# A four-layer graph network on one core: the order of the first statistics, and the last four batches' attention by another division of engines

## The chip, the cores and the metric

The kernel runs on one core of a Trainium2 chip. A core has five engines that run side by side, each with its own queue in program order: TensorE (PE in the profile, with its weight loads as PEld), VectorE (DVE), ScalarE (ACT), GpSimd (POOL) and SyncE (SP), which here only issues DMA transfers. The metric is the device time of one execution in microseconds, the median of several runs. Before the change it is 1679.53 us (3 runs, 1678.21 to 1679.84).

## The reference

There are 32 batches of 512 nodes with 128 features each (`x`), and one sparse symmetric 512x512 matrix `adj`. Four layers follow each other, each of the form `x = x + layer(...)`:

```python
# layer 0: graph convolution, out of h = relu(layernorm(x))
A_hat = adj + eye(n)
d = sum(A_hat, -1) ** -0.5
out = einsum('nm,bmc->bnc', d[:, None] * A_hat * d[None, :], h) @ W.T + b

# layer 1: gated recurrence, 5 steps from h = relu(layernorm(x)); both matrices are adj
m_in = m_out = einsum('nm,bmd->bnd', adj, h)
av = concatenate([m_in, m_out], -1)
u3 = h @ u3_w.T + u3_b
z = sigmoid(av @ w3_w.T + w3_b + u3)
r = sigmoid(av @ w4_w.T + w4_b + u3)
hv = tanh(av @ w5_w.T + w5_b + (r * h @ u5_w.T + u5_b))
h = (1 - z) * h + z * hv

# layers 2 and 3: attention over the edges, from relu(layernorm(x))
h = einsum('bnf,fo->bno', relu_ln_x, W)
e = leaky_relu((h @ a_src)[:, :, None] + (h @ a_dst)[:, None, :], 0.2)
alpha = softmax(where(edge, e, -inf), -1)
out = einsum('bij,bjo->bio', alpha, h)        # layer 2 ends in elu(out)
```

As both halves of `av` are the same, the kernel uses the sum of the two halves of `w3_w`, `w4_w` and `w5_w`.

## The kernel before

The kernel records its operations, each with an engine, an estimated cost, a due time and the values it reads and writes. A small list scheduler then runs the records through a model with those costs, deals out buffers, and emits the instructions of each engine in the order that comes out. The costs and due times are therefore part of the program: changing them changes the order on all engines, not only near the change.

```python
DELAY = {"PE": 0.25, "ACT": 0.2, "DVE": 0.15, "POOL": 0.15, "SP": 2.4, "AQ": 2.4}
...
}, 172, 0.1)                     # how urgent an operation with a long tail becomes
MM, MM1, TURN = 0.86, 0.235, 0.117
V, A = 0.61, 0.62
```

At the start, `adj` is turned, its degrees are summed, `anT` (the normalised matrix of layer 0) is made, and then the factors of `adj` that the recurrent layer's product uses. That product takes two batches at once and seven instead of eight block products; its factors are sums and differences of `adj`'s quarters.

```python
for c in range(C):               # C = 4 chunks of 128 rows
    op("PE", C * TURN, -800, turn_adj, r=[adj_sb[c], ident], w=[p])
    op("ACT", A, -800, ... nc.scalar.copy(adjT.t[:, :, c * P:(c + 1) * P], p.t) ...)
    op("DVE", V, -800, ... nc.vector.reduce_sum(deg.t[:, c:c + 1], adj_sb.t[:, c, :]) ...)
op("DVE", 0.1, -799, ... add 1 to deg)
op("POOL", 1.0, -1000, ... dinv = deg ** -0.5)
op("PE", C * TURN, -798, turn_dinv, r=[dinv, ident], w=[drow])

def scale_rows():                # one operation: four rows, then four diagonals
    for m in range(C):
        nc.vector.scalar_tensor_tensor(anT.t[:, m, :], adjT.t[:, m, :], dinv.t[:, m:m + 1], flat(drow.t), ...)
    for m in range(C):
        nc.vector.scalar_tensor_tensor(block(anT.t, m), ident.t, dinv2.t[:, m:m + 1], block(anT.t, m), ...)
op("DVE", 4 * 0.7 + 4 * 0.25, -797, scale_rows, ..., w=[anT])

half_adj = fixed([P, 7, 2, 2 * P], "half_adj", 7)
# factors 0, 3, 5: copies of quarters; 2, 1, 4, 6: differences; all on DVE, due -795
...
ws = ...                         # w4, w3, w5: halves added on DVE, then w3 - w4; PE turns the sums
```

Layer norm and the first layer:

```python
def norm_stats(b, due):          # bn_stats x4, bn_aggr x4, +eps on DVE; power -0.5 on POOL
def norm_relu(b, y, due):
    mv, rstd = norm_stats(b, due)
    op("DVE", ... off = -mean * rstd)
    for c in range(C):
        op("ACT", 0.32, due, ... nc.scalar.activation(chunk(y, c), xb.t[:, c, :], AF.Relu,
                                                      bias=off..., scale=rstd...))

def gcn(b, due):                 # called with due = 5 b - 10 or so
    norm_relu(b, y, due)
    op("DVE", V, due + 1, ... x += b0)
    m = product(y, anT, due + 1) # four 128x512 matmuls and a copy by ACT
    op("PE", C * MM1, due + 2, out_mm, ...)
    op("DVE", V, due + 2, ... x += result)
```

Attention, for the last four batches (`near`), which turn their tile on PE where the other batches go through DRAM:

```python
norm_relu(b, y, due)
if near:
    pT = to_features(y, due + 1, gT)                         # PE turns y
    op("DVE", V, due + 1, ... nc.vector.tensor_copy(gT, pT))
else:
    shuttle(y, ...)
for a in range(2):
    op("PE", 2 * MM1, due + 1.5, heads, ...)                 # h and its scores
    op("ACT", 0.1, due + 1, ... exp of the scores)
    op("DVE", 0.335, due + 1.5, ... nc.vector.tensor_mul(h, q, exp))
if near:
    op("PE", C * TURN, due + 2, spread, ...)                 # scores of all nodes on every partition
    op("ACT", A, due + 2, ... copy to row)
for j in range(C):
    op("DVE", 0.68, due + 3, ... e[j] = max(row, score j) * mask)
for a, p in enumerate(ps):
    for c in range(2):
        def mix(...):                                        # one receiving chunk, all four senders j
            for j in range(C):
                nc.tensor.matmul(..., e.t[:, j, i * P:(i + 1) * P], h.t[:, j, :D + 1], start=(j == 0), stop=(j == C - 1))
        op("PE", C * MM1, due + 4, mix, r=[e, h], w=[p])
    op("DVE", ... reciprocal of the sums)
    # layer 2: v = p * rden on DVE, then exp on ACT and two DVE operations for elu
    # layer 3: x = p * rden + x on DVE, then the write to DRAM
```

Of the kernel before, what the change touches and what calls it, by code (L numbers as in the profile page):

```python
# [12 lines left out]
ALU = mybir.AluOpType  # L13
# [29 lines left out]
class Plan:  # L43
# [3 lines left out]
    DELAY = {"PE": 0.25, "ACT": 0.2, "DVE": 0.15, "POOL": 0.15, "SP": 2.4, "AQ": 2.4}  # L47
# [104 lines left out]
def gnn_stack(ctx: ExitStack, tc: tile.TileContext, a: dict, out: bass.AP):  # L152
# [47 lines left out]
    }, 172, 0.1)  # L200
    op = plan.op
    MM, MM1, TURN = 0.86, 0.235, 0.117
    V, A = 0.61, 0.62
# [27 lines left out]
    for c in range(C):  # L231
        e, q = (("SP", nc.sync), ("ACT", nc.scalar))[c % 2]
        op(e, 0.9, -1001, lambda c=c, q=q: q.dma_start(adj_sb.t[:, c, :], adj[c * P:(c + 1) * P, :]),
           w=[adj_sb[c]], delay=2.6 + c)
# [10 lines left out]
    op("DVE", 0.25, -800, lambda: nc.vector.tensor_scalar_add(b0.t, b0.t, -1.0), w=[b0])  # L245
# [15 lines left out]
    adjT = Val("e", C)  # L261
    deg, dinv = fixed(SMALL, "deg", C), fixed(SMALL, "dinv")
    for c in range(C):
# [7 lines left out]
        op("DVE", V, -800, lambda c=c: nc.vector.reduce_sum(deg.t[:, c:c + 1], adj_sb.t[:, c, :], axis=mybir.AxisListType.X),  # L271
# [5 lines left out]
    anT = fixed([P, C, N], "anT")  # L277
# [12 lines left out]
    def scale_rows():  # L290
        for m in range(C):
            nc.vector.scalar_tensor_tensor(anT.t[:, m, :], adjT.t[:, m, :], dinv.t[:, m:m + 1], flat(drow.t),
                                           op0=ALU.mult, op1=ALU.mult)
        for m in range(C):
            nc.vector.scalar_tensor_tensor(block(anT.t, m), ident.t, dinv2.t[:, m:m + 1], block(anT.t, m),
                                           op0=ALU.mult, op1=ALU.add)
    op("DVE", 4 * 0.7 + 4 * 0.25, -797, scale_rows, r=[adjT, dinv, drow, ident, dinv2], w=[anT])


    half_adj = fixed([P, 7, 2, 2 * P], "half_adj", 7)  # L300
# [4 lines left out]
    def factor(k, out_of, *also):  # L305
        op("DVE", 0.62, -795, lambda: out_of(half_adj.t[:, k]), r=[adjT, *[half_adj[i] for i in also]], w=[half_adj[k]])
    for k, u, n in ((0, 0, 0), (3, 1, 0), (5, 1, 1)):
        factor(k, lambda o, u=u, n=n: nc.vector.tensor_copy(o, quarter(u, n)))
    factor(2, lambda o: nc.vector.tensor_sub(o, quarter(0, 1), quarter(0, 0)))
    factor(1, lambda o: nc.vector.tensor_sub(o, quarter(1, 1), half_adj.t[:, 2]), 2)  # L310
    factor(4, lambda o: nc.vector.tensor_sub(o, quarter(1, 1), quarter(0, 1)))
    factor(6, lambda o: nc.vector.tensor_sub(o, quarter(1, 0), half_adj.t[:, 1]), 1)
# [24 lines left out]
    ws = {k: fixed([P, D], k + "s") for k in ("w4", "w3", "w5")}  # L337
    for k in ("w4", "w3", "w5"):
        op("DVE", 0.25, -700, lambda k=k: nc.vector.tensor_add(ws[k].t, raw[k].t[:, :D], raw[k].t[:, D:]),
           r=[raw[k]], w=[ws[k]])  # L340
    op("DVE", 0.25, -699, lambda: nc.vector.tensor_sub(ws["w3"].t, ws["w3"].t, ws["w4"].t), r=[ws["w4"]], w=[ws["w3"]])

    def transposed(due, *group):

        p = Val("bank")
        t = fixed([P, len(group), P], "wT")

        def turns():
            for i, (v, _) in enumerate(group):
                nc.tensor.transpose(p.t[:, i, :], v.t[:, :D], ident.t)  # L350
        op("PE", len(group) * TURN, due, turns, r=[ident] + [v[0] for v, _ in group], w=[p])
# [7 lines left out]
    w0T = transposed(-750, (w0, 1))  # L359
    gates = transposed(-700, (ws["w4"], 1), (raw["u3"], 1), (ws["w3"], 1), (ws["w5"], 1))  # L360
    u5T = transposed(-690, (raw["u5"], 0.5))
    gats = transposed(-10, (w_aug[2], 1), (w_aug[3], 1))
    gate_b = {}
    for k, u, half in (("w4", "u3", True), ("w3", "u3", True), ("w5", "u5", False)):
        gate_b[k] = fixed([P, 1], "gate_b" + k)
        op("DVE", 0.1, -695, lambda k=k, u=u: nc.vector.tensor_add(gate_b[k].t, raw["b" + k].t, raw["b" + u].t),
           r=[raw["b" + k], raw["b" + u]], w=[gate_b[k]])
        if half:
            op("DVE", 0.1, -695, lambda k=k: nc.vector.tensor_scalar_mul(gate_b[k].t, gate_b[k].t, 0.5), w=[gate_b[k]])
# [26 lines left out]
    def norm_relu(b, y, due):  # L396
# [5 lines left out]
        for c in range(C):  # L402
            op("ACT", 0.32, due, lambda c=c: nc.scalar.activation(  # L403
                chunk(y, c), xb.t[:, c, :], AF.Relu, bias=off.t[:, c:c + 1], scale=rstd.t[:, c:c + 1]),
               r=[xb[c], off, rstd], w=[y[c * len(y.writers) // C]])

# [41 lines left out]
    def product(h, mT, due):  # L448

        p, m = Val("bank"), Val("m")  # L450
        for c in range(C):
            op("PE", MM, due, lambda c=c: nc.tensor.matmul(flat(p.t), chunk(h, c), mT.t[:, c, :], start=(c == 0), stop=(c == C - 1)),  # L452
               r=[h[c] if len(h.writers) > 1 else h, mT], w=[p, m])
# [4 lines left out]
    def gcn(b, due):  # L458
        xb, y = xs[b], Val("y", C)
        norm_relu(b, y, due)  # L460
# [30 lines left out]
    def products(h1, h2, due):  # L491
# [20 lines left out]
        def times(r, item, k, fresh, *also):  # L512
            def two():
                u = part(item).rearrange("p (f l) -> p l f", l=2)
                for l in range(2):
                    nc.tensor.matmul(flat(r.t)[:, :2 * P], u[:, l, :], half_adj.t[:, k, l, :], start=fresh and l == 0, stop=l == 1,  # L516
                                     skip_group_check=not fresh)
            op("PE", HM, due, two, r=[item, half_adj], w=[r, *also])
# [78 lines left out]
    def gat(b, l, due):  # L597
        xb, y, gT, h = xs[b], Val("y", C), Val("gT"), Val("h_gat", 4)
        norm_relu(b, y, due)
# [3 lines left out]
        if near:  # L603
            pT = to_features(y, due + 1, gT)
            op("DVE", V, due + 1, lambda: nc.vector.tensor_copy(
                gT.t.rearrange("p q (c i) -> p q c i", c=C), pT.t.rearrange("p c (q i) -> p q c i", q=Q)), r=[pT], w=[gT])
        else:
# [114 lines left out]
```

## Time and profile before

| | us |
|---|---|
| time, median of 3 | 1679.53 |
| span of the profiled execution | 1677.5 |
| busy PE, DVE, ACT, POOL | 1647.4, 1373.7, 675.1, 142.9 |
| first matmul of the first product of layer 0 | 21.29 |
| first matmul of the recurrent product | 37.49 |
| last addition of a recurrent result into x ends | 1619.1 |
| VectorE's last instruction ends | 1674.1 |

The profile's page gives the busy time of each engine over the whole span; its stages give the same for a stretch of time. The timeline lists instructions in order of time. A line L516 is line 516 of the kernel before; the important ones are L268 (turning adj), L283 (turning dinv), L292 and L295 (anT), L308 to L312 (the factors), L339 and L341 (weight sums), L386, L390 and L393 (statistics of the layer norm), L403 (its activation), L452 (product with anT), L516 (recurrent product), L575 (last addition of the recurrence for the last pair), L605 (copy of the turned tile), L618 (heads), L622 (scaling of h), L632 and L634 (row of scores), L647 (e) and L658 (mix). An fp32 matmul has two records on PE, a turn has one. The busy time of a stage has to be read beside the engine that feeds it: an engine that is full in one stage and half idle in another has different meaning in each.

### The profile page before, as it was taken

The page shows a single profiled execution, that of the slowest core. Times are in us where ns is not written, and L with a number is a line of the kernel's source. Part 1 is how long each engine was busy: PE and PEld are TensorE (multiplying, and loading weights), DVE is VectorE, ACT ScalarE, POOL GpSimd, SP SyncE. Part 2 cuts the span into 40 slices and gives each one's busy share as a digit, 9 for nine tenths or more (in the row PEclk, how much of TensorE's full clock was granted, in tenths as well). Part 3 has the DMA queues.
Part 4 walks back from the last instruction along what each step waited for, and adds up shares of the span by engine and source line. Part 5 has one row for each costly group of instructions (what it writes and reads, how often), then busy time and mean ns, then how long its engine had stood idle before and what let it go on. Part 6 is the DMA issues. An engine that isn't in the chain of part 4 may idle for free.

```text
span 1677.5 us, 23419 instructions
## 1 busy us (share of the span) xinstructions
PE 1647.4 (98%) x7224; PEld 1140.3 (68%) x7224; DVE 1373.7 (82%) x3894; ACT 675.1 (40%) x1458; POOL 142.9 (9%) x136
## 2 busy tenths in 40 slices
PE   6999999999999999999999999999999999999997
PEld 4656667576676676767676676776767767676786
DVE  7867688688887897969988688896978879887887
ACT  4434343525444344342543434344343434334332
POOL 2200001001010010100101010010100001000000
PEclk9999999999999999999999999999999999999999
DMA  5213333242433334243433333424233432424101
GB/s 160 52 40 76 76 88 76 69 130 73 114 88 85 103 97 101 59 105 101 125 83 83 94 94 80 112 75 120 73 95 98 110 83 79 113 76 108 45 14 32
DMA packets 311422, 146.15 MB, mean 87 GB/s; under 512 B 150400, under 2 KB 292864, under 8 KB 311296
## 3 DMA queue, kind: packets, MB, share of 16 engines
q1 hardware_dynamic: 311008, 144.12, 33.9%
q8 instruction: 57, 0.93, 0.2%
q14 instruction: 69, 0.57, 0.1%
q10 hardware_dynamic: 288, 0.52, 0.1%
HBM read 80.48 MB, written 64.08 MB: 86 GB/s over the span
## 4 chain that ended last, share of the span: by engine, by line
PE 95%; DVE 3%; ACT 1%; issue 0%; DMA 0%; POOL 0%; DVEq 0%
PE bank L516 29%; PE bank L658 13%; PE bank L545 8%; PE bank L546 8%; PE bank L552 8%; PE bank L559 8%; PE bank L560 8%; PE bank L452 7%; PE bank L618 3%; PE bank L468 2%; PE bank L419 1%; DVE e L647 1%; PE bank L639 0%; DVE st L386 0%; ACT y L403 0%
## 5 line engine op out<-in xcount | busy, mean ns | idle before, releaser
L516 PE MATMUL bank<-half_adj,S 128*128 128x256 f32 x1280 | 311.1, 380 | 1.3 <-DVE S L503 1.3
L516 PEld LDWEIGHTS bank<-half_adj,S 128*128 128x128 f32 x1280 | 245.3, 196 | 53.3 <-issue 21.1
L393 POOL TENSOR_TENSOR rstd<-ve,mhalf 128x4 f32<-128x4 f32 x128 | 140.4, 1099 | 1497.5 <-DVE ve L391 1186.3
L658 PEld LDWEIGHTS bank<-h_gat,e 128*128 128x128 f32 x2048 | 237.8, 191 | 16.0 <-issue 9.1
L516 PE MATMUL bank<-half_adj,h 128*128 128x256 f32 x960 | 243.6, 380 | 0.9 <-ACT h L579 0.5
L658 PE MATMUL bank<-h_gat,e 128*128 128x129 f32 x2048 | 240.9, 275 | 1.0 <-DVE e L647 0.9
L548 ACT ACTIVATE r<-bank,gate_bw 128x512 f32<-128x512 f32 x160 | 109.7, 685 | 288.8 <-PE bank L546 257.8
L516 PEld LDWEIGHTS bank<-half_adj,h 128*128 128x128 f32 x960 | 183.0, 196 | 39.6 <-issue 18.4
L647 DVE SCALAR_TENSOR_TENSOR e<-row,h_gat,maskT 128x512 f32<-128x512 f32 x256 | 181.0, 742 | 0.1
L403 ACT ACTIVATE y<-x,off,rstd 128x128 f32<-128x128 f32 x384 | 160.3, 484 | 50.8 <-DVE off L400 29.2
L550 DVE SCALAR_TENSOR_TENSOR rh<-r,hT 128x512 f32<-128x512 f32 x160 | 109.8, 687 | 85.6 <-ACT r L548 84.7
L564 DVE TENSOR_TENSOR hv<-hv,hT 128x512 f32<-128x512 f32 x160 | 109.1, 682 | 80.8 <-ACT hv L562 80.3
L545 PE MATMUL bank<-m,wT 128*128 128x512 f32 x320 | 163.7, 593 | 0.3 <-DVE m L536 0.3
L552 PE MATMUL bank<-m,wT 128*128 128x512 f32 x320 | 163.6, 593 | 0.0
L559 PE MATMUL bank<-m,wT 128*128 128x512 f32 x320 | 163.4, 592 | 0.0
L546 PE MATMUL bank<-hT,wT 128*128 128x512 f32 x320 | 163.4, 592 | 0.0
L560 PE MATMUL bank<-rh,wT 128*128 128x512 f32 x320 | 163.4, 592 | 0.0
L562 ACT ACTIVATE hv<-bank,gate_bw 128x512 f32<-128x512 f32 x160 | 109.5, 684 | 133.1 <-PE bank L560 131.0
L554 ACT ACTIVATE z<-bank,gate_bw 128x512 f32<-128x512 f32 x160 | 109.4, 684 | 102.9 <-PE bank L552 96.6
L452 PE MATMUL bank<-anT,y 128*128 128x512 f32 x256 | 125.2, 605 | 3.9 <-ACT y L403 3.9
L386 DVE BATCH_NORM_STATS2 st<-x 128x6 f32<-128x128 f32 x512 | 121.6, 279 | 3.0 <-DMA x<-in_x_dram 2.3
L560 PEld LDWEIGHTS bank<-rh,wT 128*128 128x128 f32 x320 | 60.8, 190 | 76.5 <-issue 68.6
(109 smaller groups left out, 1845.7 us busy)
## 6 DMA issues: line engine op xcount, KB each, us to landing
far<-sq SPq DMA_DIRECT2D x832, 64.0 KB
h<-far SPq DMA_DIRECT2D x248, 128.0 KB
gT<-far SPq DMA_DIRECT2D x56, 256.0 KB
row<-line SPq DMA_DIRECT2D x56, 256.0 KB
x<-in_x_dram SPq DMA_DIRECT2D x32, 256.0 KB
out_dram<-x SPq DMA_DIRECT2D x32, 256.0 KB
h<-far SPq DMA_DIRECT2D x28, 256.0 KB
far_mask<-mask SPq DMA_DIRECT2D x8, 128.0 KB
```

Of the source, the lines that this page charges most:

```text
L386: op("DVE", 0.21, due, lambda c=c: nc.vector.bn_stats(st.t[:, c, :], xb.t[:, c, :]), r=[xb[c]], w=[st[c]])
L393: op("POOL", 1.0, due, lambda: nc.gpsimd.tensor_tensor(rstd.t, ve.t, mhalf.t, ALU.pow), r=[ve, mhalf], w=[rstd])
L403: op("ACT", 0.32, due, lambda c=c: nc.scalar.activation(chunk(y, c), xb.t[:, c, :], AF.Relu, bias=off.t[:, c:c + 1], scale=rstd.t[:, c:c + ...
L452: op("PE", MM, due, lambda c=c: nc.tensor.matmul(flat(p.t), chunk(h, c), mT.t[:, c, :], start=(c == 0), stop=(c == C - 1)), r=[h[c] if len ...
L516: nc.tensor.matmul(flat(r.t)[:, :2 * P], u[:, l, :], half_adj.t[:, k, l, :], start=fresh and l == 0, stop=l == 1, skip_group_check=not fresh)
L545: nc.tensor.matmul(flat(gate.t), gates.t[:, 0, :], flat(m.t), start=True, stop=False)
L546: nc.tensor.matmul(flat(gate.t), gates.t[:, 1, :], flat(hT.t), start=False, stop=True)
L552: op("PE", MM, due + 0.3, lambda: nc.tensor.matmul(flat(gate.t), gates.t[:, 2, :], flat(m.t), start=False, stop=True, skip_group_check=Tru ...
L559: nc.tensor.matmul(flat(cand.t), gates.t[:, 3, :], flat(m.t), start=True, stop=False)
L560: nc.tensor.matmul(flat(cand.t), u5T.t[:, 0, :], flat(rh.t), start=False, stop=True)
L647: op("DVE", 0.68, due + 3, lambda j=j: nc.vector.scalar_tensor_tensor(e.t[:, j, :], row.t, h.t[:, j, D + 1:D + 2], maskT[l].t[:, j, :], op ...
L658: nc.tensor.matmul(pt()[:, c, :D + 1], e.t[:, j, i * P:(i + 1) * P], h.t[:, j, :D + 1], start=(j == 0), stop=(j == C - 1))
```

## The change

What it does:

- The statistics and the activation of the first two batches are due ahead of the factors of adj; the factors come later on VectorE.
- anT is made chunk by chunk, row and diagonal together, and a product's matmul waits for its chunk alone.
- The three factors that were copies of quarters are read from the turned adj in place.
- The sums of the weights' halves are no longer added on VectorE: PE accumulates the halves, turned by a product with the identity (or with minus the identity for w3 - w4).
- The last four batches: the layer norm's scaling goes to VectorE without the relu, the relu goes into the copy of the turned tile, which moves to ScalarE, and so does the scaling of h.
- Their mix runs sender by sender, so that it can begin with the first quarter of e and has little left after the last.
- The scheduler's costs, delays and two constants of urgency are set anew.

The purpose is to begin the first products earlier, to take work off VectorE at both ends, and to shorten what stands behind the last e. The diff, cut to its core:

```diff
-    DELAY = {"PE": 0.25, "ACT": 0.2, "DVE": 0.15, "POOL": 0.15, "SP": 2.4, "AQ": 2.4}
+    DELAY = {"PE": 0.24, "ACT": 0.15, "DVE": 0.12, "POOL": 0.1, "SP": 2.4, "AQ": 2.4}
-    }, 172, 0.1)
+    }, 174, 0.08)
-    MM, MM1, TURN = 0.86, 0.235, 0.117
-    V, A = 0.61, 0.62
+    MM, MM1, TURN = 0.858, 0.224, 0.111
+    V, A = 0.61, 0.585
...
-    adjT = Val("e", C)
+    adjT = fixed([P, C, N], "adjT", C)
-        op("DVE", V, -800, ... reduce_sum
+        op("DVE", 0.66, -801, ... reduce_sum
...
-    anT = fixed([P, C, N], "anT")
+    anT = fixed([P, C, N], "anT", C)
-    op("DVE", 4 * 0.7 + 4 * 0.25, -797, scale_rows, r=[adjT, dinv, drow, ident, dinv2], w=[anT])
+    for m in range(C):
+        op("DVE", 0.7, -797, ... row m, r=[adjT, dinv, drow], w=[anT[m]])
+        op("DVE", 0.26, -797, ... diagonal m, r=[ident, dinv2], w=[anT[m]])
...
-    half_adj = fixed([P, 7, 2, 2 * P], "half_adj", 7)
+    half_adj = fixed([P, 4, 2, 2 * P], "half_adj", 4)
+    PLAIN = {0: (0, 0), 3: (1, 0), 5: (1, 1)}
+    def right(k):
+        return quarter(*PLAIN[k]) if k in PLAIN else half_adj.t[:, FACTOR[k]]
-    factor(...)                  # three copies, four differences, due -795
+    for k, u, v in ((2, (0, 1), 0), (1, (1, 1), 2), (4, (1, 1), None), (6, (1, 0), 1)):
+        op("DVE", 0.62, -6, ... tensor_sub
...
-    op("DVE", 0.25, -700, ... ws[k] = raw[k][:, :D] + raw[k][:, D:]     # three, and one difference
+    minus = fixed([P, P], "minus")
+    op("ACT", 0.25, -900, lambda: nc.scalar.mul(minus.t, ident.t, -1.0), r=[ident], w=[minus])
-                nc.tensor.transpose(p.t[:, i, :], v.t[:, :D], ident.t)
+                for k, (v, at, sign) in enumerate(parts):
+                    nc.tensor.matmul(p.t[:, i, :], v.t[:, at:at + D], sign.t, start=k == 0, stop=k == len(parts) - 1)
...
+    def norm(b, y, due):
+        mv, rstd = norm_stats(b, due)
+        for c in range(C):
+            op("DVE", 0.16, due, ... nc.vector.tensor_scalar(y.t[:, c, :], xb.t[:, c, :], mv.t[:, c, 0:1], rstd.t[:, c:c + 1],
+                                                             op0=ALU.subtract, op1=ALU.mult))
...
-               r=[h[c] if len(h.writers) > 1 else h, mT], w=[p, m])
+               r=[h[c] if len(h.writers) > 1 else h, mT[c]], w=[p, m])
-        norm_relu(b, y, due)
+        norm_relu(b, y, due if b > 1 else 2 * b - 798)
...
         if near:
+            norm(b, y, due)
-            op("DVE", V, due + 1, ... tensor_copy(gT, pT))
+            op("ACT", A, due + 1, ... activation(gT, pT, AF.Relu))
...
+            if near:             # scaling of h
+                op("ACT", 2 * 0.385, due + 1.5, ... two nc.scalar.mul)
+            else:
                 op("DVE", 0.335, due + 1.5, ... tensor_mul)
...
+        if near:
+            for j in range(C):
+                def mix_from(j=j):
+                    for c in range(C):
+                        nc.tensor.matmul(... chunk c of bank c // 2 ..., e.t[:, j, c * P:(c + 1) * P], h.t[:, j, :D + 1],
+                                         start=j == 0 and c % 2 == 0, stop=j == C - 1, skip_group_check=True)
+                op("PE", C * MM1, due + 4, mix_from, r=[e[j], h[j // 2], h[2 + j // 2]], w=[*ps])
```

## The prediction

> **What bounds the kernel now.** I read the page's busy times first, then the same by stages, then PE's waits, then the timeline of the two ends.
>
> ```profile
> PE 1647.4 (98%) x7224; PEld 1140.3 (68%) x7224; DVE 1373.7 (82%) x3894; ACT 675.1 (40%) x1458; POOL 142.9 (9%) x136
> ```
>
> PE is idle for only 1677.5 - 1647.4 = 30.1 us. The stages say where (per stage: length, then busy us and instructions of PE, PEld, DVE, ACT, POOL, then PE's clock, DMA share, GB/s):
>
> ```profile
> 0.00:20.00 20.00, 8.01 (x32) 6.34 (x32) 13.12 (x49) 5.23 (x10) 2.91 (x9) 1.00 0.77 218
> 20.00:40.00 20.00, 18.71 (x61) 10.47 (x62) 17.05 (x90) 11.27 (x28) 7.59 (x8) 1.00 0.40 117
> 40.00:60.00 20.00, 20.00 (x78) 13.07 (x77) 19.36 (x86) 15.16 (x35) 7.25 (x7) 1.00 0.12 34
> ...
> 300.00:500.00 200.00, 200.00 (x890) 139.24 (x890) 166.66 (x465) 82.50 (x182) 15.87 (x15) 1.00 0.39 99
> ...
> 1619.10:1647.40 28.30, 20.60 (x171) 19.17 (x169) 27.74 (x105) 9.55 (x23) 4.88 (x5) 0.96 0.04 11
> 1647.40:1655.20 7.80, 7.52 (x44) 6.92 (x44) 4.49 (x13) 6.10 (x20) 1.60 (x2) 0.70 0.00 0
> 1655.20:1674.20 19.00, 17.11 (x144) 16.34 (x144) 16.73 (x42) 2.01 (x5) 0.00 (x0) 1.00 0.15 43
> ```
>
> From 21.3 to 1516 us PE never stops, so nothing done there can pay except less PE work, and the change does not reduce PE work. What can be had lies in the first 21 us and in the last 58. From 1619.1, where the last recurrent step adds into x, VectorE is nearly full (27.74 of 28.3) and PE is not: the end is VectorE's. PE's longest waits agree:
>
> ```profile
> PE bank L618 <- DVE gT L605: 7.2, 2, 6.7
> PE bank L268 <- DMA e<-in_adj_dram: 4.7, 1, 4.7
> PE bank L452 <- ACT y L403: 3.9, 1, 3.9
> PE bank L350 <- DMA a_pair<-in_L_gnn_a_dst_dram: 2.8, 1, 2.8
> ```
>
> The start in the timeline (start, us from first start to last end, engine, line, operation). L274 is dinv, L283 its turn, L292 anT's rows, L390 the aggregation of batch 0's statistics, L393 its power, L452 the first product:
>
> ```profile
> 9.42 1.66 POOL L274 TENSOR_TENSOR dinv<-deg,mhalf 128x4 f32<-128x4 f32 x1 [8.06 <-DVE deg L273]
> 11.32 1.06 PE L283 MATMUL bank<-ident,dinv 128*128 128x128 f32 x4
> 12.41 2.72 DVE L292 SCALAR_TENSOR_TENSOR anT<-e,dinv,bank 128x512 f32<-128x512 f32 x4 [0.47 <-PE bank L283]
> 18.84 0.37 DVE L390 BATCH_NORM_AGGREGATE mv<-st 128x2 f32<-128x6 f32 x4
> 19.50 1.01 POOL L393 TENSOR_TENSOR rstd<-ve,mhalf 128x4 f32<-128x4 f32 x1 [8.43 <-DVE ve L391]
> 21.29 8.41 PE L452 MATMUL bank<-anT,y 128*128 128x512 f32 x12 [3.93 <-ACT y L403]
> ```
>
> anT is done at 16.2, but batch 0's statistics stand in VectorE's queue behind the factors of adj, so the product waits until 21.29.
>
> **What the skill says.** "TensorE: Matmul & The Clock Gate", part 1, "The HAM clock gate": PE runs at half rate until about 3.4 us of sustained work, and falls back after an idle window. The trace agrees: weight loads of the first product come 0.855 us apart until 27.4 us and 0.43 after it; after the hole before 1647.49 eight 131-wide matmuls take 2.12 us, later eight take 1.06. So each hole costs twice. "VectorE: DVE Perf Modes", "Mode 2x_2P": single-source fp32 operations inside SBUF run at twice the rate, those on PSUM do not. Agrees: the 128x512 copy in SBUF took 421 ns, from PSUM 686. "ScalarE: Activation LUTs", "What ACT_TABLE_LOAD costs": 186 ns + 0.83 ns a column, 93 more per pointer operand; for 128 columns and two pointers 479, and the trace has 484. "PSUM", "The four PSUM rules": the first matmul of a group clears the accumulate bits of its whole bank. That is why the mix by sender starts only the first group of each bank; no run here shows it and no time hangs on it.
>
> **The start, step by step.** Back-to-back distances from the timeline: turn 0.217 cold and 0.11 warm; fp32 matmul two records, so 128 wide 0.43 cold and 0.22 warm, 512 wide 1.71 and 0.857; VectorE 128x512 with two tensors 0.6 to 0.68, bn_stats 0.2, aggregation of four 0.3. In the changed order the four degree sums stand together: 4.61 + 4 x 0.61 = 7.1. With 1.66 for the power dinv is there at 9.1 instead of 11.1. But PE's order is 16 turns of adj (4.72 to 8.2; each in a bank of its own, so the two waits of 0.7 for ScalarE go), then w0 and the sums of w4, w3 and w5, nine matmuls, and only then dinv's turns. Cold that is 3.9 + 0.9, until 13.0; if the clock opens at about 10, until 11.6. I take 12.1: drow is hardly earlier than now (12.4). The weight sums take back what the earlier dinv gave; they are 13 matmuls for 8 turns, 18 records more, 2 to 4 us of PE, at a time when PE would mostly wait.
>
> Then anT 0, off, anT 1, two diagonals: 0.68 + 0.1 + 0.68 + 0.5, so chunks 0 and 1 are there at 14.05, chunks 2 and 3 at 15.9. Batch 0's power runs right after dinv's (9.1 to 10.1), ScalarE has copied the weights by 13.2, and y's first chunk is there at 13.6. First product 14.05 to 17.6, warm if the unbroken work from 4.72 opened the clock. That is 7.2 us earlier in its start. The gain is not kept whole: VectorE, dense from here on, now has the statistics of batch 1, gate sums and factors to do, and PE is fed in pieces. Following the two orders: batch 1's product 19.2 to 23.1, its output matmuls 23.8 to 24.7, the first recurrent product 25.7 (now 37.49), and by 39.5 PE has done 21.7 us of full-speed work since its first product. Now it has done 3.05 by 27.4 and as much as 21.7 at 46.0. Gain 6.5. A check by VectorE: it is idle 10.5 us of the first 60; the change takes 4 weight sums (1.0) and 3 copies (1.2 to 1.6) off it, and about 7 us of idle time stay (the load, the wait for drow). So at most 6. I take **-5**.
>
> **The last four batches.** Per such attention layer VectorE loses the copy from PSUM (0.6), two scalings (0.66) and off (0.1) and gains four normalisations of 128 columns (about 0.14 each: the one 128x128 tensor_scalar kept the next waiting 0.13). So -0.8. ScalarE loses four activations (1.65) and gains one PSUM copy (0.6) and four scalings (some 0.4 each): +0.5, and it is idle there. Mix by sender: after the last e only 4 matmuls remain (0.9) where 13 of 16 did (2.9).
>
> VectorE's work behind the last add into x, from the changed order: 27 e x 0.665 = 18.0; 16 last additions x 0.26 = 4.2; 20 bn_stats 3.9; 20 normalisations 2.8; 6 half products x 0.33 = 2.0; 6 of elu x 0.6 = 3.6; 14 reciprocals 1.1; aggregations and eps 2.3. Sum 37.9; the same sum for now gives 47.9 against 48.96 measured, so 38.7. For waits I find 1.2 (row of the second last layer-2 batch: ScalarE's scalings stand ahead of the row copy), 0.7 and 1.7 (rows of layer 3, the same cause), in all 3.6. So 42.3 us from the last add to VectorE's end, now 55.1: -12.8. Against it: PE has 359 records (40.2 us) behind that add now and 316 (35.4) then. The 4.8 us stand ahead of it, where PE is idle 3.6 us between 1500 and 1619; I let the add come 3.5 later for this. That leaves -9; with a wait or two that I did not see, **-8**. The last write, 3.3 us, stays.
>
> **The middle.** The whole order is dealt anew because costs, delays and the urgency constants changed. Work per batch is the same (the products read adj's quarters in place, 256 columns in a run as in the copies). PE can only lose: **+1**.
>
> Sum: 1679.5 - 5 - 8 + 1 = 1667.5.
>
> **The rivals.** (1) The weight sums keep drow back: clock cold, w5 late, drow at 13, product cold (6.9 us for the first batch). For it: PE stayed cold until 21 now, though with holes. Then the start gains 2, total 1670.5. (2) ScalarE becomes the bound at the end: its queue is in order, and exp, scalings, gT and rows of three batches share it; each scaling ahead of a row delays four e's. For it: at the end some 12 us of its work stand before the last row. Against it: 17.7 busy of 55 now. Then the end gains 4, total 1671.5. (3) The new order opens holes in the middle: VectorE is busy 83% there, and a buffer handed out in another order can stall PE; 0.5% more would be +8 and eat most of it. Against it: PE had none over 1480 us. (4) Both ends come out whole: -6.5 and -12, 1661.
>
> **Range and chances.** Two ends with 2 to 4 us of doubt each and the middle with 2 to 5 on the bad side: 1660 to 1675. PE's busy time sets a floor near 1640, so 2% (1645.9) is out of reach; 2% slower would need a new stall of 45 us. 0.01, 0.98, 0.01.
>
> **What will show it.** First product of batch 0 before 15 us and its clock; dinv's turns after the weight sums, at 11.5 to 13; first recurrent product at 25 to 28. From the last add to VectorE's end 42 to 46 us, no hole of 6.7 us in PE before the last layer's heads, clock there warm. PE idle under 1 us in all between 60 and 1500. The prediction is wrong if the middle shows PE waits of several us, or if drow comes after 14.

## The result, and the profile after

| | before | after |
|---|---|---|
| time, median of 6 runs each, taken in turns on one chip | 1679.68 us | 1668.3 us |
| span of the profiled execution | 1677.5 | 1667.2 |
| first matmul of the first product | 21.29 | 13.57 |
| first matmul of the recurrent product | 37.49 | 25.20 |
| PE idle up to 60 us | 13.28 | 7.37 |
| PE idle from 60 to 1500 us | 0 | 0 |
| PE idle from 1500 us to the end of the span | 16.8 | 14.4 |
| last addition of a recurrent result into x ends | 1619.2 | 1618.58 |
| VectorE's last instruction ends | 1674.1 | 1663.85 |

The ratio after to before is 0.9935, with a 95% interval of 0.9922 to 0.9948. The prediction of 1667.5 us is 0.8 us off. That is not yet a proof of its reasons: it is a sum of three terms, and two wrong terms can cancel.

The stages of the profile after, in the columns used before the change:

```profile
0.00:20.00 20.00, 13.70 (x65) 10.49 (x66) 12.96 (x48) 9.04 (x20) 3.79 (x10) 1.00 0.76 217
20.00:40.00 20.00, 18.94 (x78) 12.45 (x77) 19.47 (x96) 10.90 (x27) 6.20 (x6) 1.00 0.41 119
...
60.00:1500.00 1440.00, 1440.00 (x6173) 989.93 (x6172) 1182.45 (x3255) 585.67 (x1235) 111.68 (x100) 1.00 0.36 90
```

and the last part of it, cut at the last addition into x and at VectorE's last instruction:

```profile
1500.00:1618.58 118.58, 114.78 (x564) 82.19 (x563) 95.80 (x268) 44.73 (x106) 8.83 (x8) 0.99 0.22 58
1618.58:1663.85 45.27, 38.02 (x303) 34.94 (x302) 40.77 (x134) 16.70 (x50) 5.57 (x5) 0.96 0.07 20
```

The middle is as full as it was: PE is busy for all of its 1440 us. Over the span PE's idle time falls from 30.1 to 21.8 us (1667.2 - 1645.4), and its busy time by 2.0, of which the lines below show a part to be cold matmuls that are now warm. Of the 8.3 us of idle time 5.9 lie in the first 60 us and 2.4 behind 1500.

The start, PE and the power of dinv in the timeline after (L347 turns weights, L283 dinv, L464 is the first product, L528 the recurrent one; in brackets the idle time ahead and what ended it):

```profile
7.61 1.02 POOL L274 TENSOR_TENSOR dinv<-deg,mhalf 128x4 f32<-128x4 f32 x1 [6.25 <-DVE deg L273]
8.04 2.20 PE L347 MATMUL bank<-ident,w 128*128 128x128 f32 x10
10.07 0.61 PE L347 MATMUL bank<-minus,w 128*128 128x128 f32 x4
...
10.97 0.60 PE L283 MATMUL bank<-ident,dinv 128*128 128x128 f32 x4
13.57 3.80 PE L464 MATMUL bank<-anT,y 128*128 128x512 f32 x8 [1.55 <-DVE anT L294]
25.20 1.48 PE L528 MATMUL bank<-adjT,h 128*128 128x256 f32 x4 [0.29 <-ACT h L406]
```

PE works without a break from 4.52 us to the end of dinv's turns. The rows show the clock open: ten records take 2.20 us at first, four then 0.61, and eight 512-wide records of the product 3.80, where twelve took 8.41 before. What the product waits for is anT's first chunk, no longer the statistics.

The waits of PE after, over the whole span (total us, times, longest):

```profile
PE bank L268 <- DMA e<-in_adj_dram: 4.5, 1, 4.5
PE bank L676 <- DVE e L667: 2.8, 3, 1.8
...
PE bank L464 <- DVE anT L294: 1.6, 1, 1.6
```

The hole of 6.7 us ahead of the last layer's heads is gone, and so is the 3.9 ahead of the first product. The heads are not warm, though, as the prediction had expected: from 1644.11 us eight of their matmuls take 1.61 us, where eight take 1.06 from 1651.40. The first row is the load of adj, which the change doesn't touch; the largest wait left at the end is the mix waiting for an e.

### The profile page after: what moved, and what is told of

The parts are those of the page before. It is cut to its first block, busy times and chain, and to the rows that moved or that the text cites. A ratio compares the mean times of both kernels' runs of the same rounds, so it can differ in the third digit from the quotient of the medians.

```text
span 1667.2 us, 23457 instructions
## 1 busy us (share of the span) xinstructions
PE 1645.4 (99%) x7242; PEld 1141.2 (68%) x7242; DVE 1371.1 (82%) x3887; ACT 681.1 (41%) x1467; POOL 143.4 (9%) x136
## 4 chain that ended last, share of the span: by engine, by line
PE 96%; DVE 3%; ACT 1%; issue 0%; DMA 0%; DVEq 0%; ACTq 0%
PE bank L528 29%; PE bank L687 11%; PE bank L557 8%; PE bank L571 8%; PE bank L572 8%; PE bank L558 8%; PE bank L564 8%; PE bank L464 6%; PE bank L632 3%; PE bank L480 2%; PE bank L676 1%; PE bank L431 1%; DVE st L389 0%; PE bank L659 0%; DVE e L667 0%; DVE y L415 0%
## 5 line engine op out<-in xcount | busy, mean ns | idle before, releaser
L528 PE MATMUL bank<-half_adj,S 128*128 128x256 f32 x960 | 239.6, 381 | 2.2 <-DVE S L515 1.8
L687 PEld LDWEIGHTS bank<-h_gat,e 128*128 128x128 f32 x1792 | 208.6, 191 | 19.4 <-issue 12.8
L528 PEld LDWEIGHTS bank<-half_adj,S 128*128 128x128 f32 x960 | 186.1, 197 | 44.2 <-issue 21.4
L687 PE MATMUL bank<-h_gat,e 128*128 128x129 f32 x1792 | 209.3, 275 | 0.7 <-ACT row L654 0.7
L528 PE MATMUL bank<-adjT,h 128*128 128x256 f32 x640 | 164.9, 380 | 0.8 <-ACT half L538 0.5
L406 ACT ACTIVATE y<-x,off,rstd 128x128 f32<-128x128 f32 x352 | 148.2, 483 | 33.0 <-DVE sq L445 17.0
L528 PEld LDWEIGHTS bank<-adjT,h 128*128 128x128 f32 x640 | 122.0, 196 | 35.3 <-issue 16.9
L464 PE MATMUL bank<-anT,y 128*128 128x512 f32 x256 | 122.7, 593 | 1.6 <-DVE anT L294 1.6
```

Source lines behind the costliest of these rows:

```text
L406: op("ACT", 0.385, due, lambda c=c: nc.scalar.activation(chunk(y, c), xb.t[:, c, :], AF.Relu, bias=off.t[:, c:c + 1], scale=rstd.t[:, c:c ...
L528: nc.tensor.matmul(flat(r.t)[:, :2 * P], u[:, l, :], right(k)[:, l, :], start=fresh and l == 0, stop=l == 1, skip_group_check=not fresh)
L687: nc.tensor.matmul(pt()[:, c, :D + 1], e.t[:, j, i * P:(i + 1) * P], h.t[:, j, :D + 1], start=(j == 0), stop=(j == C - 1))
```

## The experiments

All medians below are of runs taken in turns with the kernel before, whose median was between 1679.04 and 1679.10 in these three groups; for the changed kernel it was 1679.68. The intervals of single kernels are about 1 to 2 us to either side, so two kernels that differ by under 2 us are not told apart.

| kernel | us | ratio to before, 95% interval |
|---|---|---|
| constants alone | 1679.36 | 1.0002 (0.9994 to 1.001) |
| constants + start | 1673.09 | 0.9966 (0.9954 to 0.9979) |
| constants + end | 1676.21 | 0.9982 (0.9975 to 0.9989) |
| after, mix by receiver | 1674.88 | 0.9977 (0.9968 to 0.9985) |
| after, row ahead of the scalings | 1670.06 | 0.9947 (0.9935 to 0.996) |
| after, scaling of h on VectorE | 1667.83 | 0.9932 (0.9919 to 0.9946) |
| after, normalisation on ScalarE | 1668.35 | 0.9939 (0.9927 to 0.9952) |
| constants + start + mix by sender | 1668.74 | 0.9938 (0.9925 to 0.995) |
| after, dinv's turns first | 1666.74 | 0.9926 (0.9913 to 0.9938) |
| after, weight sums on VectorE | 1673.23 | 0.9958 (0.9944 to 0.9971) |
| after, statistics late | 1673.97 | 0.9965 (0.9952 to 0.9977) |
| after, mix by sender in layer 2 only | 1669.66 | 0.9941 (0.9929 to 0.9954) |

### Taking the change apart: constants, start, end

The theory was the prediction's: start -5, end -8, the rest +1. The first rival says that one of the ends carries nearly all of it.

**Constants alone.** The kernel before with the new delays, urgency constants and costs (those of adj's load and of the layer norm's activation are not shown).

```diff
-    DELAY = {"PE": 0.25, "ACT": 0.2, "DVE": 0.15, "POOL": 0.15, "SP": 2.4, "AQ": 2.4}
+    DELAY = {"PE": 0.24, "ACT": 0.15, "DVE": 0.12, "POOL": 0.1, "SP": 2.4, "AQ": 2.4}
-    }, 172, 0.1)
+    }, 174, 0.08)
-    MM, MM1, TURN = 0.86, 0.235, 0.117
-    V, A = 0.61, 0.62
+    MM, MM1, TURN = 0.858, 0.224, 0.111
+    V, A = 0.61, 0.585
...
```

> The kernel before with the change's scheduler constants alone (costs, delays, urgency). Theory: both ends are what was changed and the constants only re-deal a middle that is full anyway: within 2 us of the kernel before. Rival (the constants are the change): 1672 or less, with the start at 21 us and the end's 55 us as before.

Measured 1679.36: nothing. The order is dealt anew all the same: the last addition into x ends at 1625.3 instead of 1619.2, and the stretch behind it shrinks from 54.9 to 49.4 us, with no change of the time. The work behind it shrinks too: PE has 304 records there instead of 359, VectorE 44.25 us instead of 48.96. So the length of the stretch behind that cut is no measure of the end by itself; what it loses can stand ahead of it.

**Constants + start.** With the constants, all of the change up to and including layer 0: chunks of anT, factors read in place, weight sums by PE, the early statistics.

```diff
-    op("DVE", 4 * 0.7 + 4 * 0.25, -797, scale_rows, r=[adjT, dinv, drow, ident, dinv2], w=[anT])
+    op("DVE", 0.7, -797, ... row m, w=[anT[m]])
+    op("DVE", 0.26, -797, ... diagonal m, w=[anT[m]])
-        norm_relu(b, y, due)
+        norm_relu(b, y, due if b > 1 else 2 * b - 798)
...
```

> The changed start and constants, with the old attention of the last four batches. By the prediction's terms the start is worth 5 us: 1674 to 1676. By the idle and cold time of PE in the first 60 us of the two traces it is worth 8: 1670 to 1673. Rival (a lead won at the start is eaten by VectorE before 100 us): 1678 or more.

**Constants + end.** With the constants, the last four batches alone (norm on VectorE, relu in ScalarE's copy, scaling on ScalarE, mix by sender).

```diff
+            norm(b, y, due)
-            op("DVE", V, due + 1, ... tensor_copy(gT, pT))
+            op("ACT", A, due + 1, ... activation(gT, pT, AF.Relu))
+                op("ACT", 2 * 0.385, due + 1.5, ... two nc.scalar.mul)
+                op("PE", C * MM1, due + 4, mix_from, r=[e[j], h[j // 2], h[2 + j // 2]], w=[*ps])
...
```

> The changed last four batches and constants, with the old start. By the prediction's terms the end is worth 8 us: 1671 to 1673. If the start is worth 8, then only 3 to 4 are left for the end, because work and holes ahead of the last add take back what is won behind it: 1675 to 1677. In both cases VectorE's end lies 44 to 47 us behind the last add into x.

Measured 1673.09 and 1676.21. With the constants alone and the whole change that is a square of four:

| | old end | new end | the end brings |
|---|---|---|---|
| old start | 1679.36 | 1676.21 | -3.15 |
| new start | 1673.09 | 1668.3 | -4.79 |
| the start brings | -6.27 | -7.91 | |

Both ends carry, and the start carries more, close to the second reading in either expectation (1670 to 1673, and 1675 to 1677). In all four kernels PE is busy for 1440.00 of the 1440 us from 60 to 1500.

### What of the end carries it

**Mix by receiver.** The changed kernel with the old order of the mix; everything else stays.

```diff
-        if near:
+        if False:
             ... mix_from, sender by sender
-            for c in range(2 if not near else 0):
+            for c in range(2):
```

> The changed kernel with the mix by receiver again. Theory: behind the last e of a tile 13 matmuls (2.9 us) remain for 4 (0.9), and PE is what ends last in the end of the changed kernel, so 1 to 3 us slower, 1669.5 to 1671.5. Rival: PE has 16 matmuls to do either way and works through the queue of three tiles; the order within a tile costs nothing: within 1 us of the changed kernel.

Measured 1674.88: 6.6 us are given back, more than twice what the theory expected, and the kernel is no better than the start without any new end (1673.09). So the end's gain goes with the order of sums, which the prediction had named in one sentence. Among PE's waits of this kernel a new one comes right behind the load of adj, the turn of the normalised tile:

```profile
PE bank L431 <- DVE y L415: 4.5, 2, 3.7
```

The stages of this kernel, cut at its last addition, at the last normalisation of layer 3 and at VectorE's end:

```profile
1617.24:1651.89 34.65, 27.03 (x199) 24.08 (x199) 29.75 (x105) 13.44 (x38) 5.54 (x5) 0.95 0.05 16
1651.89:1669.16 17.27, 15.21 (x110) 14.19 (x109) 12.32 (x31) 2.79 (x8) 0.00 (x0) 0.90 0.11 32
```

and of the changed kernel, cut at the same three events:

```profile
1618.58:1648.71 30.13, 24.46 (x185) 21.71 (x185) 28.80 (x105) 12.16 (x35) 5.57 (x5) 0.94 0.04 11
1648.71:1663.85 15.14, 13.56 (x120) 13.22 (x118) 11.97 (x31) 4.54 (x15) 0.00 (x0) 1.00 0.14 40
```

Layer 2 takes 34.65 us by receiver and 30.13 by sender, layer 3 takes 17.27 and 15.14. VectorE's work hardly differs between the two (42.07 and 40.77), its share falls. PE's busy time differs by 4.2 us with five records more, and the timeline of PE, mix by receiver, says why:

```profile
1621.48 2.18 PE L431 MATMUL bank<-ident,y 128*128 128x128 f32 x8 [3.67 <-DVE y L415]
1623.45 1.93 PE L687 MATMUL bank<-h_gat,e 128*128 128x129 f32 x8
...
1652.96 2.11 PE L632 MATMUL bank<-w_aug,gT 128*128 128x131 f32 x8 [0.69 <-ACT gT L617]
...
1665.13 3.17 PE L687 MATMUL bank<-h_gat,e 128*128 128x129 f32 x26 [0.17 <-DVE e L667]
```

PE is empty for 3.67 us and comes back at half the rate: eight turns take 2.18 us and eight 129-wide matmuls 1.93, and later, behind another hole, eight 131-wide ones 2.11, where each of these takes about 1.1 in the warm rows of the changed kernel. That makes some 3 us, but the changed kernel has cold rows of its own around 1645 us. The clock is either full or half in these traces, so the clock columns above give the time at half rate: 2 x (0.05 x 34.65 + 0.10 x 17.27) = 6.9 us here and 2 x 0.06 x 30.13 = 3.6 in the changed kernel. The 3.3 us between them can cost PE at most 1.7 of the 4.2. The last row is the lump of the prediction: by receiver 3 of a batch's 16 matmuls run under the last e's, one each, and 13 (26 records, 3.17 us) stand behind the last of them. The mix of the changed kernel, beside VectorE's e:

```profile
1653.55 5.39 DVE L667 SCALAR_TENSOR_TENSOR e<-row,h_gat,maskT 128x512 f32<-128x512 f32 x8 [2.10 <-ACT row L654]
1654.06 8.20 PE L676 MATMUL bank<-h_gat,e 128*128 128x129 f32 x72
```

Here PE works under the e's in one unbroken row. But it isn't done with them: an e takes VectorE 0.67 us and its four matmuls PE 0.9, and two batches' e's come back to back, so at the last e's end (1658.94) PE has 3.3 us left, to 1662.26. By receiver those are 3.2 (1665.08 to 1668.30). In the last group of layer 2 the same count gives 1.9 by sender (1638.76 to 1640.66) and 3.2 by receiver (1641.11 to 1644.34). Behind the very last e, then, nothing is gained; in the last group of layer 2 it is 1.3 us.

**Mix by sender alone.** The kernel with constants + start, and of the end's parts only the mix.

```diff
 # constants + start, and:
+                op("PE", C * MM1, due + 4, mix_from, r=[e[j], h[j // 2], h[2 + j // 2]], w=[*ps])
-            for c in range(2):
+            for c in range(2 if not near else 0):
```

> The changed start and constants with the old attention of the last four batches, except that the mix runs by sender. With the mix by receiver the changed kernel took 1674.9, and the changed start alone 1673.1: so the moves to ScalarE without the mix are worth nothing. Theory: the mix carries the end's gain alone: 1667 to 1669.5. Rival: the two need each other (VectorE relieved, then PE's leftover is what shows): 1671 to 1673.

Measured 1668.74 against 1668.3 of the whole change. The other three parts of the end, all that moves work between VectorE and ScalarE, are worth nothing that can be seen. Nor does the gain come from a clock that stays open. From the last addition to VectorE's end, constants + start have this stage:

```profile
1618.28:1667.55 49.27, 41.19 (x304) 37.37 (x304) 44.23 (x136) 13.93 (x38) 5.52 (x5) 0.93 0.08 22
```

and with the mix by sender alone added (from 0.6 us ahead of the last addition's end):

```profile
1616.84:1663.95 47.11, 38.38 (x290) 36.21 (x288) 42.31 (x135) 15.07 (x41) 6.06 (x5) 0.89 0.08 21
```

The clock is at half rate for longer by sender, 2 x 0.11 x 47.11 = 10.4 us against 2 x 0.07 x 49.27 = 6.9, and the kernel is 4.4 us faster all the same.

**Which layer.** Mix by sender in layer 2, by receiver in layer 3.

```diff
-        if near:
+        if near and l == 2:
-            for c in range(2 if not near else 0):
+            for c in range(2 if not (near and l == 2) else 0):
```

> The changed kernel with the mix by sender in layer 2 alone, by receiver in layer 3. Theory: the end is the dependent chain of the last pair (statistics to e to mix, twice), and each mix by sender takes 2 us off that chain; so layer 3 alone is worth 2 to 3 of the 6.6 us: 1670 to 1671.5. Rival: only the very end counts, where nothing hides what PE has left after the last e: nearly all of it, 1673.5 to 1675. Second rival: only layer 2 counts, as layer 3's tiles queue behind each other on PE anyway: within 1 us of the changed kernel.

Measured 1669.66. Of the 6.6 us layer 2 carries 5.2 and layer 3 1.4, the latter within the uncertainty. That fits the counts above in its place, though not in its size (1.3 us in one group): what is saved is saved in layer 2, where a batch's mix stands ahead of its own layer 3. Here too the clock isn't the reason: from the last addition to VectorE's end its mean is 0.93, as it is with the mix by receiver.

### Is the end VectorE's, or ScalarE's?

**Scaling of h on VectorE.** This puts eight scalings of 128x256 per attention layer back on VectorE.

```diff
-            if near:
+            if False:
                 def scale(qt=qt, ht=ht):
```

> The changed kernel with the scaling of h back on VectorE (two of 0.33 us a tile for ScalarE's four of 0.3). Theory (VectorE is the bound of the end): about 8 tiles x 0.66 = 5 us more on VectorE, of which 2 to 4 show: 1670 to 1672.5. Rival (chains and PE bound the end, not VectorE's sum): within 1.5 us of the changed kernel, or faster as rows come sooner.

**Normalisation on ScalarE.** Layer norm by ScalarE's activation as before, for the last four batches; the relu in the copy stays, and has no effect there.

```diff
         if near:
-            norm(b, y, due)
+            norm_relu(b, y, due)
```

> The changed kernel with the layer norm of the last four batches on ScalarE again (four activations of 0.41; the copy of the turned tile stays there too). The normalisation on VectorE took 0.26 us a piece in the trace, not the 0.14 of the prediction: 20 of them behind the last add are 5.3 us. Theory (VectorE's sum): up to 3 us faster, 1665 to 1668. Rival (latency: four in a row on a ScalarE that also has exp, rows and scalings, 1.65 for 1.05, plus the off): 1 to 3 slower, 1669.5 to 1671.5.

Measured 1667.83 and 1668.35: both as the changed kernel, the second between its two forecasts. Yet from 1500 us on VectorE is busy for 136.6 us in the changed kernel, 141.1 with the scalings back on it and 131.1 without the normalisations. The largest part of the last is this group of VectorE behind the last addition, here in the changed kernel (busy us, mean ns of one, idle time before):

```profile
L415 DVE TENSOR_SCALAR y<-x,mv,rstd 128x128 f32<-128x128 f32 x20 | 5.8, 337 | 0.0
```

So the sum of VectorE's work does not set the length of the end: 4.6 us more or 5.5 less leave the time as it was. Both runs hand work from one engine to the other, so a gain on one may be taken back on the other: with the scalings on VectorE its idle time behind the last addition is 2.6 us (44.17 - 41.60), where it is 4.5 in the changed kernel.

**Row ahead of the scalings.** The rival in which ScalarE's queue, in order, holds the rows back: here the scalings of h are recorded behind the copy of the row and wait for it.

```diff
+            for a, q in enumerate(qs):
+                def scale(a=a, q=q):
+                    for c in range(2):
+                        nc.scalar.mul(...)
+                op("ACT", 2 * 0.3, due + 1.5, scale, r=[q, h[2 + a], row], w=[h[a]])
```

> The changed kernel, but in the last four batches ScalarE copies the row of scores before it scales h (the scalings wait for the row). Theory, rival 2 of the prediction: e of a tile waits for the row behind up to four scalings (2.1 us before the e of the last two tiles in the trace), so 1 to 3 us faster than the changed kernel, 1665.5 to 1667.5. Rival: at the end PE has 64 mix records in a row (7.2 us) and is the bound, so the earlier e only waits elsewhere: within 1 us.

Measured 1670.06, no gain. VectorE's waits of the changed kernel from 1600 us on show 2.1 us of e waiting for the row and 2.1 of the reciprocals waiting for the mix. In this kernel the first is gone, and the second has grown:

```profile
DVE rden L691 <- PE bank L677: 4.3, 3, 3.9
```

So with the row's wait gone VectorE waits for the mix instead. In part the edit brings this itself: the mix reads the scaled h, which now comes after the row, and PE waits 1.3 us for it. The run shows that this order gains nothing, and not what the row's wait costs by itself.

### What of the start carries it

**Statistics late.** The changed kernel, with the first two batches' statistics and the factors due as before.

```diff
-    op("DVE", 0.62, -6, ... tensor_sub
+    op("DVE", 0.62, -795, ... tensor_sub
-        norm_relu(b, y, due if b > 1 else 2 * b - 798)
+        norm_relu(b, y, due)
```

> The changed kernel with the factors due ahead of the statistics again, as before; anT by chunks, weight sums by PE and the end stay. Theory: the order of the statistics is most of the start's 6 to 8 us; the first product at 18 to 20 us and 4 to 6 us slower, 1672 to 1674. Rival (VectorE's sum in the first 60 us decides, and it is the same): within 2 us.

Measured 1673.97: 5.7 us of the start's 6 to 8 are gone. Its first product, in its timeline:

```profile
19.01 8.29 PE L464 MATMUL bank<-anT,y 128*128 128x512 f32 x12 [1.68 <-ACT y L406]
```

It starts 5.4 us later than in the changed kernel, again behind y, and after PE had stood empty before it, its first part is cold: from 10 to 20 us the mean granted clock is 0.73.

**Weight sums on VectorE.** The changed kernel with the sums back on VectorE and turned by a transpose each, so that PE has 18 records less.

```diff
+    op("DVE", 0.25, -700, ... nc.vector.tensor_add(ws[k].t, raw[k].t[:, :D], raw[k].t[:, D:]) ...
-                for k, (v, at, sign) in enumerate(parts):
-                    nc.tensor.matmul(p.t[:, i, :], v.t[:, at:at + D], sign.t, start=k == 0, stop=k == len(parts) - 1)
+                nc.tensor.transpose(p.t[:, i, :], v.t[:, :D], ident.t)
```

> The changed kernel with the weights' halves added on VectorE and turned, as before. Theory: the sums on PE did two things, they spared VectorE 1.1 us and they kept PE at work from 4.5 to 12 us, so that its clock opened near 10 us. Without them PE has holes, the first product (3.4 us of full-speed work) runs cold in part, 1.5 to 3 us, and VectorE has 1.1 more in its dense stretch: 1670 to 1672. Rival (holes under 2 us close nothing, and drow is earlier): within 1 us of the changed kernel.

Measured 1673.23: slower by 4.9 us (3.9 by the ratios of the table), more than either forecast. The timeline of PE shows that the theory of rival 1 is right as to order and wrong as to cost:

```profile
8.36 0.42 PE L350 MATMUL bank<-ident,w 128*128 128x128 f32 x1
9.49 0.62 PE L283 MATMUL bank<-ident,dinv 128*128 128x128 f32 x4 [0.72 <-ACT wT L354]
...
12.12 5.37 PE L461 MATMUL bank<-anT,y 128*128 128x512 f32 x8 [1.81 <-DVE anT L294]
...
26.50 2.08 PE L525 MATMUL bank<-adjT,h 128*128 128x256 f32 x4 [1.46 <-ACT h L403]
```

Without the sums dinv is turned 1.5 us earlier and the product starts 1.45 us earlier. But it takes 5.37 us for eight records, not 3.80, and the recurrent product starts 1.3 us later. The cold product only gives back what its early start had won: batch 0's output matmuls start at 18.16 us, in the changed kernel at 18.04. The loss begins at the recurrent product. Its off leaves VectorE, which here has the sums to do as well, 1.3 us later (25.75 for 24.45), PE waits 1.46 us for h where it waited 0.29, and then the first four records take 2.08 us, where four take 1.03 once the clock is open. So a closed clock and a later h stand side by side, and this run doesn't part them. The stages from 10 to 20 us, first of this kernel:

```profile
10.00:20.00 10.00, 8.17 (x27) 4.22 (x26) 8.12 (x29) 4.40 (x11) 1.09 (x1) 0.83 0.73 188
```

then of the changed kernel:

```profile
10.00:20.00 10.00, 8.22 (x42) 5.26 (x41) 8.02 (x27) 4.74 (x12) 1.01 (x1) 1.00 0.72 187
```

PE is busy as long in both, with 27 records in one and 42 in the other, and the clock column reads 0.83 and 1.00. The sums are work that PE needn't do, and they fill the holes from 8.4 to 12.1 us. "TensorE: Matmul & The Clock Gate", part 1, "The HAM clock gate", in the Trainium skill says that sustained work opens the clock; this run agrees, but the 4.9 us are not the price of the clock alone.

**dinv's turns first.** The changed kernel in which all weights' turns but the first group also read dinv, so that dinv's turns come ahead of them.

```diff
-            op("PE", len(parts) * MM1, due, turns, r=[ident, minus] + [q[0] for q in parts], w=[p[i]])
+            op("PE", len(parts) * MM1, due, turns, r=[ident, minus] + [q[0] for q in parts] + [dinv] * (due > -750), w=[p[i]])
```

> The changed kernel with the turns of dinv ahead of the weight sums on PE (gates and u5 wait for dinv). Rival 1 of the prediction: the weight sums stand between dinv (there at 8.6 in the trace) and drow (11.6). With them behind, drow comes at about 9.6 and the first product at about 11.5 to 12.5 for 13.6. Theory (PE's start sets the time): 1 to 2 us faster, 1666.3 to 1667.3. Rival (from 14 us on VectorE is full and sets the pace): within 0.7 us.

Measured 1666.74, the lowest median of all; its interval overlaps that of the changed kernel, so it beats the kernel before for sure and the changed one perhaps. Its timeline of PE:

```profile
9.46 1.08 PE L283 MATMUL bank<-ident,dinv 128*128 128x128 f32 x4 [0.47 <-ACT wT L351]
...
12.76 3.60 PE L464 MATMUL bank<-anT,y 128*128 128x512 f32 x8
```

The product starts 0.8 us earlier and warm, since the sums now lie where PE waits for anT. The order has half of the early start of the version without the sums (0.81 of 1.45 us) and the open clock of the one with them.

## Why the prediction was right in its sum, step by step

- **The middle, +1:** measured 0 (constants +0.3 in all, PE without a hole). Right; rival 3 (new holes in the middle) is out.
- **The start, -5:** measured -6.3 with the old end and -7.9 with the new. The mechanism is right: the statistics ahead of the factors (putting both back costs 5.7 us), a warm product, drow hardly earlier. The term was on the small side, by little more than the runs resolve. Its times were half a microsecond late: dinv's power took 1.02 us and not the 1.66 carried over, dinv came at 8.63 and not 9.1, the product at 13.57 and not 14.05, the recurrent one at 25.20 and not 25.7. The larger piece is probably the cap by which I held the 6.5 of PE's order down to 5, from VectorE's idle time: PE's idle time up to 60 us alone fell by 5.9.
- **Rival 1** (sums hold drow back): the order is as it said, dinv's turns stand behind the sums and lose 1.5 us by it. Its cost was not: it expected the clock cold with the sums, and it is without them that the clock closes; taking them away makes the kernel 4.9 us slower, by the clock and a later h together.
- **The end, -8:** measured -3.1 to -4.8. This is the term that failed, and the step in it is "the end is VectorE's". From VectorE's fill (27.74 of 28.3 us in one stretch of the kernel before) I took its work as the length of the end and summed that. The runs show: 5.5 us of VectorE's work handed to ScalarE, no gain; the scalings taken back from ScalarE, no loss; the mix by sender alone, the whole gain. And where the mix was spoken of, its gain was put behind the last e ("only 4 matmuls remain (0.9)"): PE had 3.3 us left there, as much as by receiver, and the gain came in layer 2. The sign "clock there warm" did not come either.
- **The sum for it** was also off in its terms. The stretch behind the last addition is 45.27 us, not 42.3: VectorE's work there is 40.77, not 38.7, chiefly because the 20 normalisations take 5.8 us and not 2.8; its waits are 4.5 and not 3.6. I had taken 0.14 for one from a 128x128 row without pointer operands; with two of them it is 337 ns, one every 0.26 us. "VectorE: DVE Perf Modes", section "The TRN2 errata", warns of a fixed cost per instruction that small tiles pay each time, and puts the fixed term of one operation at about 150 cycles by its own measurement; with 64 for 128 columns at two a cycle, (64 + 150) / 0.96 is an estimate of 223 ns from it, still a third below the 337 here; the measurement decides.
- **The stretch behind the last addition** was the wrong thing to sum. It shrank by 9.7 us (from 54.9, in the prediction 55.1, to 45.27), but the constants alone take 5.5 of that (49.4) and gain nothing: they move the last addition 6.1 us later, and with it some of the work to a place ahead of it. The correction of 3.5 for work moved ahead was meant for this, but it was laid to the end's own changes and was too small. Measured against the constants, the new end shortens the stretch from 49.4 to 46.9 us with the old start and from 49.3 to 45.3 with the new one, by 2.5 and 4.0, and the square of four gives 3.1 and 4.8. The work moved ahead filled no holes: from 1500 us to the last addition PE is idle 3.8 us (118.58 - 114.78), and was idle 3.6 before.
- **Rival 2** (ScalarE's rows): the wait is there, 2.1 us, and the one order that removes it gained nothing: VectorE then waits for PE.
- **Rival 4** (both ends whole, 1661): the start came whole, the end did not.

So the start brought 1.3 to 2.9 us more than predicted, the end 3.2 to 4.9 less, the middle cost 1 less, and the three came out within 0.8 of the sum. That they cancel so closely is luck.

What stays open is what sets the 45 us that are left behind the last addition. No engine is full there (VectorE 40.77, PE 38.02), and taking away single waits of VectorE or single work of it didn't help; a chain across three engines is what the waits suggest, and no run settled it. That the order of the mix carries the end's gain is shown, and that the clock does not; by which path the earlier results of layer 2 shorten the rest is argued from the counts, which find 1.3 us of it. Open, too, is how the 4.9 us of the weight sums divide between the clock and VectorE.

## What to carry to other kernels

A sum over tiles that come one after the other is best run in the order in which they arrive, over all receivers, and most of all where the result feeds a next layer: with the queue in order, work that waits for the last tile keeps back what stands behind it. Before counting an engine's work as the length of a stretch, take a few us of its work away in one run; an engine that looks full is not yet the bound. Work moved from VectorE into a hole of PE ahead of a long product can be a gain, though PE then has more to do, and where the cut between two stages floats with the schedule, whole times in a square of four are the measure, not the lengths of stretches.

## What the runs showed of the hardware

- The clock fell back with short holes: with the weight sums on VectorE it was open at 9.49 us, where dinv's four turns took 0.62 us as in the changed kernel (0.60) and not 1.06 as before. PE then had idle stretches of 0.72 and 1.81 us around these turns, and the first product fell to half rate soon after its start. Weight loads of that kernel's product (the first column is the start):

```profile
12.09 0.30 PEld L461 LDWEIGHTS bank<-anT,y 128*128 128x128 f32 x2 [1.97 <-ACT y L403]
12.62 0.33 PEld L461 LDWEIGHTS bank<-anT,y 128*128 128x128 f32 x1 [0.24 <-ACT y L403]
13.47 0.33 PEld L461 LDWEIGHTS bank<-anT,y 128*128 128x128 f32 x1 [0.52 <-issue]
```

  The first two come as in the changed kernel (0.30 us for both); from 12.62 they are 0.85 us apart until 16.0, and 0.43 after it. The section of the skill named above gives about 3.4 us both for the sustained work and for the idle time. The 3.4 us at half rate (12.6 to 16.0) agree with the first; as to the second, the clock closed here behind two holes well below 3.4 us.
- Turns opened the clock as well as other matmuls: in that same kernel PE had done nothing but turns, 16 of adj and one of a weight, from 4.92 us on, and the clock was open at 9.49. In the changed kernel, with turns and products with the identity from 4.52 us on, it opened at about 10.
- In the kernel before the clock column read 1.00 from 20 to 40 us, although its first product had its loads 0.855 us apart until 27.4. The spacing of records is the surer sign.
- A scaling of 128x128 from PSUM by a pointer operand on ScalarE took 368 ns, but two in a row 0.63 us, where the prediction had put some 0.4 for each.
